# Cross attention of layer 1: scores kept with keys on partitions, so that the weights need no transposing

## The chip, the cores and the metric

The kernel runs on one core of one Trainium2 chip, as one launch. The metric is device time in microseconds (us), lower is better: the median of repeated runs. The profile below is of one further execution.

## The reference

The network is a two-layer perceiver block over x of shape (16, 64, 512), with a context of (16, 1601, 512) and a mask over the 1601 keys. Layer 0 (a similarity attention, a self attention and a mixture of experts) and what follows the cross attention in layer 1 (a differential attention with a feed-forward block, then a ternary feed-forward block with a convolution) are untouched. The changed part is the cross attention of layer 1, in float32, with 16 heads of 32:

```
q = split_heads(queries @ Wq + bq)      # queries: layernorm(x), 64 rows in each of 16 batches
k = split_heads(keys @ Wk + bk)         # keys = values = ctx, 1601 rows in each batch
v = split_heads(values @ Wv + bv)
scores = einsum('bhqd,bhkd->bhqk', q, k) / sqrt(32)
scores = where(mask, -1e15, scores)
attn = softmax(scores, axis=-1)
ctx = einsum('bhqk,bhkd->bhqd', attn, v)
return ctx @ Wo + bo
```

## The kernel before

Layer 0 comes first and takes about 866 us of the span. Layer 1 is one long loop, in l1_layer. Its outer index is the batch b (16 of them), its inner index f picks one of four groups of four heads. One pass of the inner loop is called a unit here: there are 64. A unit handles four heads of one batch as two pairs (j = 0, 1); each pair has its 2 x 64 queries together, so that a tile of scores has 128 columns or rows of queries. Eight units (two batches, b even then b odd) make a cycle, since the later work of a tile of 128 rows of x (two batches) is spread over one. The units of a cycle are named U0 to U7 in this document: U0 to U3 are f = 0 to 3 of an even batch, U4 to U7 of an odd one.

In a unit of the kernel before:

- blank tiles p (128 queries x 1601 keys, one for each pair) are filled with -1e15 by GpSimd (POOL), L1182;
- scores (L815) puts queries on partitions: the block-diagonal queries qbd are the stationary operand, 64 rows of the array for each pair j, and the projected keys kT are streamed, 384 or 449 keys to a PSUM bank. The four banks of the tag "mm" take half of the keys at a time. VectorE (DVE) copies the allowed scores over the blanks (copy_predicated, L823), with the mask as uint8;
- DVE takes the maximum of each row (L1192), and ScalarE (ACT) computes the exponential with the maximum as bias and sums it in the same instruction (L1193);
- one unit later, TensorE (PE) transposes the 2 x 13 blocks of weights (transpose_keys, L182), ACT copies them out of PSUM (L185), and attend (L833) multiplies them with the values, 52 matmuls of 32 columns x 64;
- at the end of a batch, finish transposes the sums, inverts them on DVE, spreads them over partitions by matmuls with the 0/1 tile "spread" (L852), and scales the result.

Between these stand the projections of the next unit's keys (project_k, L146: 4 matmuls for each of four chunks n, copied out of PSUM by ACT at L758 into kT) and, in units of even f, of the values (project_v, L146). Steps of the later layers are interleaved: `run(behind, ...)` takes some steps of the generator later(t) after every chunk n. Their heavy part on DVE is products (L886 a product of 128 x 1024, L887 its sum over 16), 24 of these pairs in a cycle, which fall at the end of U0 and in U1 to U3. later(t) waits on the finished cross attention of the tile before.

The program is written in this order, and each engine works through a queue of its own strictly in order; a waiting instruction holds everything behind it on its engine. A scheduler of the framework fixes the order of each queue when the kernel is built: it may move an instruction ahead of others of its engine, as far as buffers and dependences allow. Buffers: four PSUM banks "mm" in turn for scores and projections, two "tp" for transposes, two "acc"; four tiles p, so that those of one unit come free when attend of that unit is done.

## Time and profile before

| | |
|---|---|
| runs (us) | 3614.35, 3618.15, 3618.94; median 3618.15 |
| profiled execution: its time, its span | 3622.86, 3621.2 |
| span to the first score of layer 1 | about 894 us |
| the 64 units | about 894 to 3405 us |
| one cycle of eight units, in the steady part | 324.3 to 326.2 us (the first cycle, with other work interleaved, 256.9) |
| rest after the last unit (the last tile's later layers) | about 216 us |
| busy share of the span: PE, PE weight loads, DVE, ACT, POOL | 91%, 61%, 45%, 31%, 10% |

A line of the profile names a line of the kernel, an engine, an operation, out<-in, partitions x elements, and a count; then the busy time in us and the mean of one in ns. A float32 matmul stands in it as two records. The granted PE clock (PEclk) is the share of full speed that the throttle allowed. The end of a matmul's record is modelled: where matmuls follow each other, the distance between starts is the time that one costs.

### The profile page before, as it was taken

The numbers are of one execution on the slowest core, as the hardware profiler recorded it, in microseconds if no ns is written. First come the engines' busy times: TensorE is split into PE (matmuls) and PEld (weight loads), VectorE is DVE, ScalarE is ACT, GpSimd is POOL, SyncE is SP. The second block draws the span as 40 slices with busy tenths as digits, with TensorE's granted clock in tenths as the row PEclk, the third lists the DMA queues.
The fourth block names the chain that finished last, engine by engine and source line by source line (L and its number), as shares of the span: only waits on it lengthen the run. The fifth ranks groups of instructions, "written<-read, shape, count | busy, mean of one in ns | idle before, by whom it ended". The sixth has DMA issues, their size and how long they took to land. (4 is left out here: it accounts for less than half of the span.)

```text
span 3621.2 us, 49699 instructions
## 1 busy us (share of the span) xinstructions
PE 3285.8 (91%) x21116; PEld 2194.4 (61%) x21116; DVE 1639.5 (45%) x2580; ACT 1139.1 (31%) x2214; POOL 377.3 (10%) x340
## 2 busy tenths in 40 slices
PE   6898998995999999999999999999999999999815
PEld 2242445583667766767676676766667766666614
DVE  2010214214443743582566249345725744581583
ACT  1111011111333334343433433343434334343402
POOL 0000001442011010011001000100110010010000
PEclk9999998997999999999999999999999999999957
DMA  9949301596421113212311322232133113213213
GB/s 357 355 160 371 124 11 57 204 347 194 143 83 58 58 57 120 92 45 88 118 47 51 115 99 65 71 109 73 39 105 112 62 48 124 93 39 100 67 35 119
DMA packets 267374, 418.03 MB, mean 115 GB/s; under 512 B 20736, under 2 KB 164224, under 8 KB 267152
## 3 DMA queue, kind: packets, MB, share of 16 engines
q1 hardware_dynamic: 254656, 370.28, 31.1%
q0 software_dynamic: 12496, 44.57, 3.6%
q8 instruction: 166, 2.72, 0.3%
q14 instruction: 56, 0.46, 0.0%
HBM read 392.26 MB, written 22.54 MB: 115 GB/s over the span
## 5 line engine op out<-in xcount | busy, mean ns | idle before, releaser
L146 PE MATMUL ps_mm<-ctxT,x1w 128*128 128x384 f32 x1536 | 555.3, 492 | 1.9 <-DVE p L823 0.2
L146 PE MATMUL ps_mm<-x1w,ctxT 128*128 128x256 f32 x2304 | 523.7, 381 | 0.0
L146 PEld LDWEIGHTS ps_mm<-x1w,ctxT 128*128 128x128 f32 x2304 | 434.4, 190 | 79.8
L823 DVE COPY_PREDICATED p<-mk,ps_mm 128x384 f32<-128x384 uint8 (+1 forms) x512 | 270.1, 595 | 356.9 <-PE ps_mm L815 356.8
L1182 POOL MEMSET p<- 128x1601 f32 x128 | 185.9, 1454 | 1852.4 <-PE ps_tp L182 1848.7
L146 PEld LDWEIGHTS ps_mm<-ctxT,x1w 128*128 128x128 f32 x1536 | 273.1, 192 | 133.6 <-DVE p L823 7.3
L185 ACT COPY pT<-ps_tp 128x512 f32<-128x512 f32 x504 | 230.4, 503 | 356.8 <-PE ps_tp L182 356.8
L773 ACT COPY v<-ps_mm 128x256 f32<-128x256 f32 (+1 forms) x416 | 152.1, 370 | 418.6 <-PE ps_mm L146 417.9
L182 PEld LDWEIGHTS ps_tp<-ident,p 128*128 128x128 f32 (+1 forms) x1768 | 200.0, 143 | 137.2 <-issue 57.6
L182 PE MATMUL ps_tp<-ident,p 128*128 128x128 f32 (+1 forms) x1768 | 256.9, 282 | 4.8 <-ACT pT L185 1.6
L1192 DVE TENSOR_REDUCE negm<-p 128x1 f32<-128x1601 f32 x128 | 226.6, 1811 | 1.2
L146 PE MATMUL ps_mm<-x1w,ctxT_last 128*128 128x256 f32 (+1 forms) x1024 | 226.2, 379 | 0.0
L886 DVE TENSOR_TENSOR prod<-qkv 128x1024 f32<-128x1024 f32 x128 | 156.6, 1223 | 138.4 <-ACT qkv L918 134.8
L1193 ACT ACTIVATE p<-p,negm 128x1601 f32<-128x1601 f32 x128 | 208.0, 1627 | 14.3 <-DVE negm L1192 13.6
L146 PEld LDWEIGHTS ps_mm<-x1w,ctxT_last 128*128 128x128 f32 (+1 forms) x1024 | 181.2, 177 | 48.5 <-issue 12.1
L146 PE MATMUL ps_mm<-ctxT_last,x1w 128*128 128x449 f32 x512 | 206.4, 540 | 0.0
L815 PE MATMUL ps_mm<-kT,qbd 64*128 64x384 f32 x768 | 197.0, 528 | 0.1
L758 ACT ACTIVATE kT<-ps_mm,cols 128x384 f32<-128x384 f32 x192 | 109.4, 578 | 206.5 <-PE ps_mm L146 206.5
L146 PEld LDWEIGHTS ps_mm<-hT,w 128*128 128x128 f32 x1024 | 132.2, 194 | 56.1 <-ACT hid L1002 40.4
L887 DVE TENSOR_REDUCE att<-prod 128x64 f32<-128x1024 f32 x128 | 155.9, 1218 | 3.7
L146 PE MATMUL ps_mm<-uT,w 128*128 128x512 f32 (+1 forms) x512 | 150.9, 456 | 7.2 <-DMA w<-in_x_Wq_dram 5.5
L146 PE MATMUL ps_mm<-hT,w 128*128 128x128 f32 x1024 | 142.6, 284 | 2.4 <-ACT hid L1002 1.0
(290 smaller groups left out, 3809.3 us busy)
## 6 DMA issues: line engine op xcount, KB each, us to landing
ctxT<-in_ctx_T_dram SPq DMA_DIRECT2D x48, 1024.0 KB, 12.5
ck<-in_ctx_dram SPq DMA_DIRECT2D x48, 1024.0 KB, 11.8
ctxT<-in_ctx_T_dram SPq DMA_DIRECT2D x48, 768.0 KB, 4.5
w<-in_W1T_dram SPq DMA_DIRECT2D x64, 512.0 KB, 4.5
w<-in_W2T_dram SPq DMA_DIRECT2D x64, 512.0 KB, 3.7
wt<-tern SPq DMA_DIRECT2D x64, 512.0 KB, 4.3
ctxT_last<-in_ctx_T_dram SPq DMA_DIRECT2D x16, 898.0 KB, 4.8
w<-in_x_Wq_dram SPq DMA_DIRECT2D x16, 512.0 KB, 4.4
```

Of the source, the lines that this page charges most:

```text
L146: g.nc.tensor.matmul(out, lhsT=lhs(c), rhs=rhs(c), start=(c == 0), stop=(c == n - 1))
L182: g.nc.tensor.transpose(pt[:kw, j, :], p[:, k0 + j * P : k0 + j * P + kw], g.ident)
L185: (out_of or (lambda o, i: evac(g, o, i)))(pT[:kw, :blocks, :], pt[:kw, :blocks, :])
L758: nc.scalar.activation(kT, ps[:, :w], AF.Identity, bias=col(g, "x1_bk", f))
L773: nc.scalar.copy(v[:kw], ps[:kw, :256])
L815: nc.tensor.matmul(bank[:, : KC[n][1]], lhsT=qbd[ts(j, 2 * HDX), f].rearrange("p j s -> p (j s)"), rhs=kTs[b, f, n][ts(j, 2 * HDX), :], st ...
L823: nc.vector.copy_predicated(ps_[j][:, k0 : k0 + w], mk[:, k0 : k0 + w], bank[:, :w])
L886: nc.vector.tensor_tensor(pr, qv.unsqueeze(2).to_broadcast([P, CH, 32, 16]), kv, ALU.mult)
L887: nc.vector.tensor_reduce(out[:, ts(i, CH * 32)], pr.rearrange("p i j d -> p (i j) d"), AX.X, ALU.add)
L1182: nc.gpsimd.memset(p, -1e15)
L1192: nc.vector.tensor_reduce(negm, p, AX.X, ALU.max, negate=True)
L1193: nc.scalar.activation(p, p, AF.Exp, bias=negm, accum_out=sums[:, 2 * f + j : 2 * f + j + 1])
```

## The change

The scores are computed transposed. The keys kT become the stationary operand, and qbd is streamed: a block of 128 keys x 128 queries for each pair, 26 matmuls in a unit in place of 8. The first eight blocks are issued where scores stood; the other five after the first chunk of project_k. The mask is transposed to the keys' side once for each batch (allowed): PE does it in bfloat16, DVE copies it back to uint8. The copy_predicated instructions take four blocks at a time, with the mask broadcast over the two heads of a pair. The tile p is then 128 keys x 13 blocks x 128 queries, and attend uses it as it stands. The 26 transposes of a unit and their copies on ACT are gone.

The softmax now runs over partitions and blocks. DVE takes the maximum over the 13 blocks (maxima); PE transposes this 128 x 128 tile for each pair; DVE takes the maximum of each row, negated, and multiplies the identity with it (minus_max); a matmul with ones spreads these values to all partitions (weights), and DVE adds them to p; ACT computes the exponential without bias or sum. The sum over the blocks is done by POOL with five additions for each pair, and the sum over partitions by four matmuls with ones in attend, which write to the second half of the bank po. finish inverts there, and the tile spread is gone. blank now takes four memsets, as the last block is only 65 keys high.

```diff
--- before.py
+++ after.py
@@ -667,7 +666,7 @@
     nc, tc = g.nc, g.tc
     wk, wv = g.wk, g.wv
-    NP = HX // 2
+    NB = len(KT)
     with ExitStack() as es:
...
-        ptpool = pool("x1_pt", 6)
...
-        spread = one.tile([NP, 2, NC, P], F32, tag="spread", name="spread")
...
@@ -793,74 +781,139 @@
             )
             qTs[t] = qT
+        def allowed(b):
+            m8 = mpool.tile([S, S2], U8, tag="m8", name="m8")
+            nc.sync.dma_start(out=m8, in_=g.mask[b])
+            mb = mpool.tile([S, S2], BF16, tag="mb", name="mb")
+            nc.vector.tensor_scalar(mb, m8, 0.0, None, ALU.is_equal)
+            pt = g.ps.tile([P, NB, S], BF16, tag="tp", name="ps_tm", bufs=g.psbufs["tp"])
+            for k, (k0, kw) in enumerate(KT):
+                nc.tensor.transpose(pt[:kw, k, :], mb[:, ds(k0, kw)], identb[:S, :S])
+            mk = mpool.tile([P, NB, S], U8, tag="mk", name="mk", bufs=2)
+            nc.vector.tensor_copy(mk[:, : NB - 1], pt[:, : NB - 1])
+            nc.vector.tensor_copy(mk[:kw, NB - 1], pt[:kw, NB - 1])
+            return mk
         def prepare(b, qT):
-            mk = mpool.tile([P, S2], U8, tag="mk", name="mk")
-            for j in range(2):
-                nc.sync.dma_start(out=mk[ts(j, S), :], in_=g.mask[b])
-            nc.vector.tensor_scalar(mk, mk, 0.0, None, ALU.is_equal)
             qbd = spool.tile([P, NC, 2, S], F32, tag="qbd", name="qbd", bufs=2)
             for j in range(2):
                 nc.vector.tensor_scalar(
                     qbd[:, :, j, :], qT[:, :, ts(b % 2, S)], parity[:, j : j + 1], None, ALU.mult
                 )
-            return mk, qbd
-        def scores(b, f, ns, ps_, mk, qbd):
...
-                k0, w = KC[n]
+            return qbd
+        def scores(b, f, blocks, ps_, mk, qbd):
+            banks = [(k, j, mm(g)) for k in blocks[::4] for j in range(2)]
+            for n in reversed(range(len(banks) // 2)):
+                for k in blocks[4 * n : 4 * n + 4]:
+                    c = min(k // 3, len(KC) - 1)
+                    at, kw = k * P - KC[c][0], KT[k][1]
+                    for j in range(2):
+                        nc.tensor.matmul(
+                            banks[2 * n + j][2][:kw, ts(k % 4, P)],
+                            lhsT=kTs[b, f, c][ts(j, 2 * HDX), ds(at, kw)],
+                            rhs=qbd[ts(j, 2 * HDX), f].rearrange("p j s -> p (j s)"),
+                            start=True, stop=True,
+                        )
+            for k, j, bank in banks:
+                n = min(4, NB - k)
+                rows = KT[k][1]
                 nc.vector.copy_predicated(
-                    ps_[j][:, k0 : k0 + w], mk[:, k0 : k0 + w], bank[:, :w]
-                )
...
-                for r in reversed(range(4)):
+                    ps_[j][:rows, k : k + n, :].rearrange("p k (h s) -> p k h s", h=2),
+                    mk[:rows, k : k + n, :].unsqueeze(2).to_broadcast([rows, n, 2, S]),
+                    bank[:rows, : n * P].rearrange("p (k h s) -> p k h s", k=n, h=2),
+                )
+        def blank():
+            p = ppool.tile([P, NB, P], F32, tag="p", name="p")
+            nc.gpsimd.memset(p[:, : NB - 1], -1e15)
+            nc.gpsimd.memset(p[: P // 2, NB - 1], -1e15)
+            nc.gpsimd.memset(p[P // 2 :, NB - 1], -FMAX)
+            nc.gpsimd.memset(p[P // 2 : KT[-1][1], NB - 1], -1e15)
+            return p
+        def maxima(ps_):
+            mx = spool.tile([P, 2, P], F32, tag="mx", name="mx")
+            for j, p in enumerate(ps_):
+                nc.vector.tensor_reduce(
+                    mx[:, j, :], p.rearrange("p k x -> p x k"), AX.X, ALU.max
+                )
+            return mx
+        def minus_max(mx):
+            pt = mm(g, tag="tp")[:, : 2 * P].rearrange("p (j x) -> p j x", j=2)
+            for j in range(2):
+                nc.tensor.transpose(pt[:, j, :], mx[:, j, :], g.ident)
+            negm = small.tile([P, 2], F32, tag="negm", name="negm")
+            nc.vector.tensor_reduce(negm, pt, AX.X, ALU.max, negate=True)
+            dg = spool.tile([P, 2, P], F32, tag="mx", name="dgm")
+            for j in range(2):
+                nc.vector.tensor_scalar(dg[:, j, :], g.ident, negm[:, j : j + 1], None, ALU.mult)
+            return dg
+        def weights(ps_, dg):
+            pb = mm(g, tag="tp")
+            nc.tensor.matmul(
+                pb[:, : 2 * P], lhsT=g.ones, rhs=dg.rearrange("p j x -> p (j x)"),
+                start=True, stop=True,
+            )
+            H = NB // 2
+            sums = []
+            for j, p in enumerate(ps_):
+                nc.vector.tensor_tensor(
+                    p, p, pb[:, ts(j, P)].unsqueeze(1).to_broadcast([P, NB, P]), ALU.add
+                )
+                nc.scalar.activation(p, p, AF.Exp)
+                s = spool.tile([P, H, P], F32, tag="sum", name="sum", bufs=3)
+                nc.gpsimd.tensor_tensor(s, p[:, :H], p[:, H : 2 * H], ALU.add)
+                nc.gpsimd.tensor_tensor(s[:, :3], s[:, :3], s[:, 3:], ALU.add)
+                for q in (s[:, 1], s[:, 2], p[:, NB - 1]):
+                    nc.gpsimd.tensor_tensor(s[:, 0], s[:, 0], q, ALU.add)
+                sums.append(s[:, 0])
+            return sums
+        def attend(b, f, ps_, po, sums):
+            for k in range(NB):
+                kw = KT[k][1]
+                for r in range(4):
                     nc.tensor.matmul(
                         po[ts(r, HDX), ts(f, S)],
                         lhsT=vs[b, f // 2, k][:, ts(4 * (f % 2) + r, HDX)],
-                        rhs=pTs[r // 2][k][:, ts(r % 2, S)],
-                        start=(k == len(KT) - 1), stop=(k == 0),
+                        rhs=ps_[r // 2][:kw, k, ts(r % 2, S)],
+                        start=(k == 0), stop=(k == NB - 1),
                     )
+            for r in range(4):
+                nc.tensor.matmul(
+                    po[ts(r, HDX), ts(NC + f, S)], lhsT=g.ones[:, :HDX],
+                    rhs=sums[r // 2][:, ts(r % 2, S)], start=True, stop=True,
+                )
         otile, qTs = {}, {}
-        def finish(b, po, rs8):
+        def finish(b, po):
             t, hb = divmod(b, 2)
-            pt = mm(g, tag="tp")
-            nc.tensor.transpose(pt[:NP, :P], rs8, g.ident)
...
-            nc.scalar.copy(rb.rearrange("p f s -> p (f s)"), pr[:, : NC * S])
+            rb = spool.tile([P, NC * S], F32, tag="rb", name="rb")
+            nc.vector.reciprocal(rb, po[:, NC * S :])
             if hb == 0:
                 otile[t] = spool.tile([P, NC, P], F32, tag="oT", name="oT")
             oT = otile[t]
             nc.vector.tensor_tensor(
                 oT[:, :, ts(hb, S)],
-                po[:, : NC * S].rearrange("p (f s) -> p f s", f=NC), rb, ALU.mult,
+                po[:, : NC * S].rearrange("p (f s) -> p f s", f=NC),
+                rb.rearrange("p (f s) -> p f s", f=NC), ALU.mult,
             )
             if hb == 0:
                 return
@@ -1172,32 +1225,13 @@
             project_k(0, 0, n)
         pending = None
         behind, asked = ternary_weights(), iter(())
+        mk_next = allowed(0)
         for b in range(B):
-            mk, qbd = prepare(b, qTs[b // 2])
+            mk, qbd = mk_next, prepare(b, qTs[b // 2])
             for f in range(NC):
                 bk, fk = divmod(b * NC + f + 1, NC)
-                ps_ = []
-                for j in range(2):
...
-                    ]
+                ps_ = [blank() for j in range(2)]
+                scores(b, f, range(8), ps_, mk, qbd)
                 before = pending
                 if b % 2 == 1 and f == 0 and b + 1 < B:
                     asked = queries(b // 2 + 1)
@@ -1205,17 +1239,24 @@
                     if bk < B:
                         project_k(bk, fk, n)
                     if n == 0:
+                        scores(b, f, range(8, NB), ps_, mk, qbd)
                         if before is not None:
-                            attend(*before[:2], pTs, before[3])
+                            attend(*before)
                             if f == 0:
-                                finish(b - 1, *before[3:])
+                                finish(b - 1, before[3])
                         if f == 0:
                             po = mm(g, tag="acc")
                             if b % 2 == 0 and b > 0:
                                 behind = later(b // 2 - 1)
-                        pending = (b, f, ps_, po, sums)
+                        mx = maxima(ps_)
+                    if n == 2:
+                        dg = minus_max(mx)
+                        if f == 2 and b + 1 < B:
+                            mk_next = allowed(b + 1)
                     if f % 2 == 0:
                         project_v(b, f // 2, n)
+                    if n == 3:
+                        pending = (b, f, ps_, po, weights(ps_, dg))
                     run(behind, 1 if f % 2 == 1 or b % 2 + f == 0 and n < 2 else 3 + f // 2)
                     if n == 3:
                         run(asked, 1)
@@ -1223,9 +1264,8 @@
                     load_ctx(b + 1)
             if b % 2 == 1:
                 run(behind)
-        pTs = [transpose_keys(g, ptpool, p) for p in pending[2]]
-        attend(*pending[:2], pTs, pending[3])
-        finish(B - 1, *pending[3:])
+        attend(*pending)
+        finish(B - 1, pending[3])
         run(later(NT - 1))
```

## The prediction, made before the changed kernel was run

> **What bounds the kernel now.** I read first the busy shares of the page, then the same shares unit by unit, then what PE waits for, then one unit in order of time. The page says that PE is the bound, and its rows by slices say that this holds from about 894 to 3405 us, where the 64 units lie, while DVE swings between one tenth and nine:
>
> ```profile
> PE 3285.8 (91%) x21116; PEld 2194.4 (61%) x21116; DVE 1639.5 (45%) x2580; ACT 1139.1 (31%) x2214; POOL 377.3 (10%) x340
> ...
> PE   6898998995999999999999999999999999999815
> ...
> DVE  2010214214443743582566249345725744581583
> ```
>
> The windows of one steady cycle, U0 to U7, each from a unit's first scores to the next unit's, show where DVE is dense (the columns are the busy us of PE, PEld, DVE, ACT and POOL, then the granted clock, the DMA share and GB/s):
>
> ```profile
> 2450.00:2510.90 60.90, 60.18 (x380) 46.13 (x377) 27.23 (x38) 19.09 (x40) 4.15 (x3) 1.00 0.31 92
> 2510.90:2532.90 22.00, 20.85 (x183) 12.48 (x182) 21.69 (x22) 10.42 (x17) 2.87 (x2) 1.00 0.13 46
> 2532.90:2579.10 46.20, 43.70 (x293) 32.28 (x290) 43.04 (x43) 16.08 (x32) 4.07 (x4) 1.00 0.23 69
> 2579.10:2599.50 20.40, 19.06 (x159) 12.03 (x160) 17.30 (x27) 9.54 (x16) 2.87 (x2) 0.83 0.06 18
> 2599.50:2669.30 69.80, 68.54 (x434) 50.55 (x433) 14.67 (x27) 23.75 (x51) 6.74 (x5) 1.00 0.24 75
> 2669.30:2701.40 32.10, 31.61 (x237) 19.34 (x237) 9.88 (x16) 13.09 (x24) 2.87 (x2) 1.00 0.42 132
> 2701.40:2752.70 51.30, 49.45 (x382) 38.50 (x381) 26.65 (x60) 26.53 (x55) 3.08 (x2) 1.00 0.29 98
> 2752.70:2776.20 23.50, 22.27 (x197) 13.59 (x196) 15.97 (x31) 10.57 (x18) 2.87 (x2) 1.00 0.23 76
> ```
>
> U1 to U3 hold most of the products. DVE is busy there for 82.0 of 88.6 us: PE and DVE are both full. Elsewhere DVE has room. What PE waits for in the steady part is small, and all of it stands at this attention:
>
> ```profile
> PE ps_acc L833 <- ACT pT L185: 22.6, 35, 1.3
> PE ps_mm L815 <- DVE p L823: 21.9, 23, 2.0
> ```
>
> **What PE gets back.** This is PE in the first part of U1 (start, us, then the instruction; x counts records, two to a float32 matmul, one to a transpose):
>
> ```profile
> 2510.95 1.67 PE L815 MATMUL ps_mm<-kT,qbd 64*128 64x384 f32 x8
> 2512.55 0.66 PE L182 MATMUL ps_tp<-ident,p 128*128 128x128 f32 x4
> ...
> 2517.73 1.04 PE L182 MATMUL ps_tp<-ident,p 128*128 128x128 f32 x8
> 2518.60 0.81 PE L146 MATMUL ps_mm<-ctxT,x1w 128*128 128x384 f32 x2
> 2519.25 0.71 PE L182 MATMUL ps_tp<-ident,p 128*128 128x128 f32 x5
> 2519.79 0.49 PE L146 MATMUL ps_mm<-ctxT,x1w 128*128 128x384 f32 x1
> ```
>
> From 2510.95 to 2519.79 are 8.84 us; two stretches of projection inside take 0.75 and 0.65, so scores and transposes cost 7.4 us with their waits. attend adds 1.6 us and a wait of 0.5. finish has 16 records of L852 at 0.125 (29.9 us for 240) and a transpose for each batch, 0.5 us a unit. Sum 10.0 us.
>
> New on PE in a unit: 52 records of scores, 128 wide. A 128-wide record on all rows costs 0.11 us (L146 hT,w: 8 in 1.05 us less the modelled end). The two pairs sit on different halves of the rows; the old scores cost 0.56 of the same width on all rows (8 records of 384 in 1.67 against 2.74 us, ends taken off). So 0.061 each, 3.2 us; bounds 2.9 and 5.7 (no overlap), taken 3.2, as weight loads of the halves already come four in 0.3 us. attend: 56 matmuls at 0.032 (104 records in 1.66 us), 1.8. Two transposes 0.2; the ones matmul, two 256-wide records at 0.22, 0.45; the mask, 13 bfloat16 transposes near 0.1 (their weight loads: 98 ns), 0.3 a unit. Sum 6.0. PE gets back 4.0 us a unit, 256 us in 64, if nothing waits. ACT loses the copies of L185, about 4 us a unit, which only PE's waits felt. SP carries one mask transfer a batch for two, issued earlier; nothing queues behind it.
>
> **What DVE pays, a unit.** Two additions of 1664 elements: 512 from PSUM cost 0.691 us (L1106), 1024 cost 1.223 (L886), so 1.04 ns an element and 1.89 us each, 3.8. The maxima: contiguous like L1192 they cost 1.88; but L1137, which reads across a stride as here, took 1.061 us for 512 against 0.668 contiguous (L1081). The 0.39 belongs to its 128 results (then 2.3 us) or to its 512 reads (3.2): I take 2.5, over 1.81 before, +1.4 for two. The second maximum 0.42 (L1142 and 128 elements more), the two diagonals 0.54 (L1064), the copies 4.3 against 4.1. Sum +6.3 us; the mask adds 1.1 a batch and now falls wholly in U2, 2.2 there.
>
> **Where it waits.** The order built for each queue is known.
>
> (a) *DVE-bound stretch.* In U1 to U3, 82.0 + 3 x 6.3 + 2.2 = 103.1 us, less half a pair of products now ahead of U1 (1.2), is 101.9 us of DVE against 88.6 us of wall: +13.3 a cycle with DVE never idle, +20 if its old 6.6 us of idleness stay. The static order puts one or two pairs of products between the maxima and the diagonals, so PE cannot run ahead.
>
> (b) *Additions before copies.* At U3/U4 and U5/U6 (U1/U2 and U2/U3 lie in (a)), PE's ones matmul is directly followed by the 16 first scores, which fill all four banks, and then by project_k, which needs a bank. The copy that frees it queues behind both additions: 0.2 + 3.8 + 0.63 less 1.95 of scores is 2.7 us of PE idle. At the other four boundaries 3.4 us or more of other matmuls stand in between. If that cover goes, 2.7 each.
>
> (c) *A bank through ACT.* The last five blocks need the bank that project_k(0) has just filled: ACT's 0.58 (L758) and the hand-over, 0.8 us in each unit outside (a).
>
> (d) *Sums on POOL.* 1536 elements for a pair at 2.46 ns (L988: 512 in 1.263; L944: 256 in 0.620), 3.8 us, two pairs 7.6, memsets about 4.2: 12 us, inside every unit. They end 11.3 us after the ones matmul, when PE has come 11 us on: nothing, but any slowing is PE's.
>
> (e) *U7*: the second maximum queues behind the ternary stage's scaling on DVE, 2 us.
>
> The Trainium skill speaks against the change here: "SBUF — State Buffer", Who interferes with whom, says that a DVE instruction with two SBUF inputs and a POOL instruction that reads SBUF exclude each other for a whole instruction. The row cannot tell: L886 lasted 1204 to 1229 ns throughout, beside a POOL that mostly only wrote. By the rule, some third of 24 products meets an addition and waits 0.6 us: 5 us a cycle, in (a), where it counts. By the row, 0. I take 5; without it the end is 35 us lower.
>
> And the clock. "TensorE: Matmul & The Clock Gate", HAM oscillation, warns of idle gaps above about 3.4 us. The trace is stricter: U3 above, with waits of 1.99 and 0.57 us, was granted 0.83, and such U3 last 19.6 to 20.4 us against 18.8 at 0.91. I price each gap of (b) at 1.2 us by the row; by the rule it would be 0, and the end 20 us lower.
>
> **The sum.** A steady cycle: U0 -3.2; U1 to U3 +13.3; U4 and U6 -4.0 + 2.7 + 0.8 = -0.5 each; U5 -3.2; U7 -1.2; clock +2.4; lock +5: +12, seven times +85. The first cycle (ternary work, U1 and U3 at 17.6 of 23.9 and 18.7 of 19.5 us of DVE): U1 +1, U3 +6, U5 and U7 +1.6 each, the even ones -0.5: +8. The tail trades transposes for the longer softmax: 0. Together +93. The profiled execution took 3622.86 us (span 3621.2), 4.7 above the median, so on the median of the runs: 3618 + 93, **3710 us**.
>
> **The rivals.**
>
> *Products give way, faster.* DVE is idle for 34 us in U0 and 55 in U4. If the products really slide there, U1 to U3 lose nothing but PE's gain: they break even once they grow by less than 8.6 us a cycle (the sum of the other five units) in place of 13.3 plus lock and clock. At zero growth, -8.6 x 7 and some 20 in the first: 3540 us; with no wait at all, 3362. Against it: the queue's order is fixed, with the pairs where they were. Chance 0.25.
>
> *No overlap of the row halves.* Scores at 5.7 us: 2.5 x 40 units outside DVE's hold, +100: 3810. Against it is the ratio 0.56. Chance 0.10.
>
> *DVE and POOL heavier.* Maxima 3.2 us (+4 a cycle), DVE's old idleness kept (+6.7), sums late by a lock on both sides: 3800. Chance 0.10.
>
> *It cancels.* Gain and waits within 0.2%, about what this measurement can tell from no change: 3615. Chance 0.05.
>
> **How the numbers follow.** The likeliest case has 0.50, its own range 3640 to 3790. Faster is the first rival and 0.02 of the likeliest, 0.27; same 0.05; slower 0.68. The range leaves out the lower part of the first rival and the upper tails: 3520 to 3830.
>
> **What would show it.** Right: L182 gone from the units; score records near 0.06 us apart; additions near 1.9 us; a cycle near 337 us, with U1 and U3 longer, U0 and U5 shorter; PE waiting at project_k for the copies, with a lower clock. Wrong: U1 to U3 not longer than 88.6 us; PE's share of the cycle still 97%; or waits of PE for POOL's sums of several us.

## The result and the profile after

The change makes the kernel slower: 3722.36 us, median of four runs (3718.62 to 3729.11), against 3616.32 us for the kernel before on the same chip. The ratio is 1.0295, with a 95% interval of 1.0276 to 1.0314. The forecast was 3710 us.

The profiled execution took 3719.31 us with a span of 3717.5, 96.3 us more span than before. (The medians lie 106 us apart: the profiled execution of the kernel before was 6.5 us above its median, this one 3.1 below.) Cut at the same instruction in each unit (the start of the unit's first maximum), those 96.3 us lie here: 0.4 ahead of the first unit, 28.3 in the first cycle (256.9 before, 285.2 after), 64.4 in the other seven (6.5 to 11.3 us each), 3.2 in the tail (216.8 before, 220.0 after).

The page's first part and its slices, of the changed kernel:

```profile
PE 3202.4 (86%) x22460; PEld 2182.1 (59%) x22460; DVE 2103.6 (57%) x2928; ACT 886.0 (24%) x1548; POOL 1024.6 (28%) x1357
...
PE   6898998995889989989988998999899989989715
...
DVE  2110214214865865794778469567846865794673
```

PE has 83 us less work in its records and DVE 464 us more; yet DVE's share of the span is only 57%. PE's row, one solid block of nines before, has eights all through the loop. The windows of one steady cycle, U0 to U7, each from 7.4 us ahead of the unit's first maximum as in the prediction's table (there that was the first scores), with the columns of the prediction's table (us, then busy time of PE, PEld, DVE, ACT and POOL, granted clock, DMA share, GB/s):

```profile
2516.60:2576.20 59.60, 56.48 (x402) 44.67 (x398) 37.43 (x45) 17.92 (x31) 25.58 (x29) 1.00 0.31 96
2576.20:2602.20 26.00, 19.92 (x206) 12.98 (x207) 25.90 (x28) 5.04 (x6) 5.03 (x9) 0.93 0.04 15
2602.20:2651.40 49.20, 42.18 (x318) 31.83 (x316) 44.23 (x45) 10.86 (x21) 13.91 (x21) 0.92 0.22 70
2651.40:2678.40 27.00, 21.12 (x216) 13.34 (x217) 25.50 (x26) 6.46 (x7) 15.45 (x21) 0.94 0.01 2
2678.40:2742.40 64.00, 62.69 (x403) 47.33 (x403) 25.08 (x42) 19.50 (x41) 22.19 (x29) 0.98 0.28 88
2742.40:2773.50 31.10, 30.14 (x272) 19.66 (x271) 15.80 (x20) 7.57 (x13) 3.89 (x8) 1.00 0.39 126
2773.50:2827.10 53.60, 48.87 (x397) 38.73 (x399) 37.68 (x72) 22.94 (x44) 12.49 (x18) 0.97 0.32 106
2827.10:2851.20 24.10, 21.47 (x221) 13.13 (x219) 20.98 (x36) 6.54 (x9) 12.26 (x19) 1.00 0.19 61
```

| unit | before | after | difference | predicted |
|---|---|---|---|---|
| U0 | 60.9 | 59.6 | -1.3 | -3.2 |
| U1 to U3 | 88.6 | 102.2 | +13.6 | +13.3, and 5 for the lock |
| U4, U5 | 101.9 | 95.1 | -6.8 | -3.7, and 1.2 for the clock |
| U6, U7 | 74.8 | 77.7 | +2.9 | -1.7, and 1.2 for the clock |
| cycle | 326.2 | 334.6 | +8.4 | +12 |

U1 to U3 carry the loss. DVE is busy for 95.6 of their 102.2 us (82.0 of 88.6 before), and at first sight step (a) is confirmed. What PE waits for in the loop and the drain behind it (us in total, times, longest) tells more:

```profile
PE ps_acc L892 <- ACT p L876: 77.6, 33, 5.2
PE ps_acc L899 <- POOL sum L881: 71.5, 46, 3.0
PE ps_mm L146 <- DVE p L826: 36.3, 36, 2.4
PE ps_tp L866 <- DVE dgm L860: 22.9, 13, 2.1
```

The exponentials, the sums and the banks come behind the matmul with ones; only the diagonals (22.9 us) lie ahead of it. Here is the end of U1 on PE, in order of time (start, us, then the instruction):

```profile
2595.09 0.70 PE L866 MATMUL ps_tp<-dgm,ones 128*128 128x256 f32 x2 [2.14 <-DVE dgm L860]
2595.72 3.38 PE L817 MATMUL ps_mm<-qbd,kT 64*128 64x128 f32 x32
2600.97 0.30 PE L892 MATMUL ps_acc<-p,v 128*32 128x64 f32 x4 [1.88 <-ACT p L876]
...
2601.71 4.23 PE L146 MATMUL ps_mm<-ctxT,x1w 128*128 128x384 f32 x8 [0.43 <-DVE p L826]
...
2610.94 0.31 PE L899 MATMUL ps_acc<-sum,ones 128*32 128x64 f32 x4 [1.52 <-POOL sum L881]
...
2643.34 2.06 PE L817 MATMUL ps_mm<-qbd,kT 64*128 64x128 f32 x32
```

and the same boundary on DVE:

```profile
2594.56 0.48 DVE L860 TENSOR_SCALAR dgm<-ident,negm 128x128 f32<-128x128 f32 x2
2594.95 1.21 DVE L940 TENSOR_REDUCE att<-prod 128x64 f32<-128x1024 f32 x1
2596.19 1.23 DVE L939 TENSOR_TENSOR prod<-qkv 128x1024 f32<-128x1024 f32 x1
2597.34 3.68 DVE L873 TENSOR_TENSOR p<-p,ps_tp 128x1664 f32<-128x1664 f32 x2
2600.93 2.58 DVE L826 COPY_PREDICATED p<-mk,ps_mm 128x512 f32<-128x512 uint8 x4
```

PE has the ones matmul done by 2595.7. DVE first finishes a product, then adds for 3.7 us, then copies. PE's next instructions are two matmuls of attend, which the scheduler put ahead of project_k: they need the exponential behind the first addition, and project_k needs the bank behind both. After the gap the same eight records of projection that otherwise take 2.74 us take 4.23, and the first scores took 3.38 us in place of the 2.06 they take at 2643.34. The granted clock says why:

```profile
2592.90:2595.10 2.20, 0.06 (x2) 0.01 (x1) 2.20 (x6) 0.64 (x1) 0.00 (x0) 1.00 0.00 0
2596.20:2599.60 3.40, 2.90 (x30) 2.60 (x26) 3.40 (x3) 0.27 (x1) 0.00 (x0) 0.50 0.00 0
2603.00:2606.40 3.40, 3.40 (x10) 1.54 (x9) 1.60 (x2) 0.36 (x1) 3.16 (x5) 0.50 0.00 0
```

In the first of these windows PE all but stands; in the other two, behind the gaps, it has half its clock.

### The profile page after: what moved, and what is told of

It is laid out like the page before. It is cut to its first block, busy times and chain, and to the rows that moved or that the text cites. A ratio compares the mean times of both kernels' runs of the same rounds, so it can differ in the third digit from the quotient of the medians.

```text
span 3717.5 us, 53532 instructions
## 1 busy us (share of the span) xinstructions
PE 3202.4 (86%) x22460; PEld 2182.1 (59%) x22460; DVE 2103.6 (57%) x2928; ACT 886.0 (24%) x1548; POOL 1024.6 (28%) x1357
## 4 chain that ended last, share of the span: by engine, by line
PE 54%; DVE 30%; DMA 6%; POOL 5%; ACT 4%; issue 2%; SPq 0%; POOLq 0%; ACTq 0%; DVEq 0%
PE ps_mm L146 36%; PE ps_acc L146 7%; DVE mx L845 6%; DVE prod L939 6%; DVE att L940 4%; PE ps_acc L1062 3%; DVE p L873 3%; DVE p L826 3%; DMA ctxT<-in_ctx_T_dram 3%; DMA ck<-in_ctx_dram 2%; POOL sum L878 2%; PE ps_mm L817 2%; DVE o L940 2%; POOL sum L881 2%; PE ps_acc L282 1%
## 5 line engine op out<-in xcount | busy, mean ns | idle before, releaser
L878 POOL TENSOR_TENSOR sum<-p 128x768 f32<-128x768 f32 x128 | 244.7, 1912 | 1126.7 <-ACT p L876 1126.7
L826 DVE COPY_PREDICATED p<-mk,ps_mm 128x512 f32<-128x512 uint8 (+1 forms) x512 | 285.1, 619 | 294.9 <-PE ps_mm L817 275.0
L845 DVE TENSOR_REDUCE mx<-p 128x128 f32<-128x1664 f32 x128 | 379.7, 2996 | 0.0
L873 DVE TENSOR_TENSOR p<-p,ps_tp 128x1664 f32<-128x1664 f32 x128 | 235.6, 1882 | 126.9 <-PE ps_tp L866 126.9
L835 POOL MEMSET p<- 128x1536 f32 x128 | 177.4, 1386 | 264.7 <-PE ps_acc L899 255.0
L876 ACT ACTIVATE p<-p 128x1664 f32<-128x1664 f32 x128 | 201.8, 1587 | 135.6 <-DVE p L873 135.0
L817 PE MATMUL ps_mm<-qbd,kT 64*128 64x128 f32 x2304 | 206.4, 294 | 10.3 <-DVE p L826 3.7
L817 PEld LDWEIGHTS ps_mm<-qbd,kT 64*128 64x128 f32 x2304 | 172.0, 198 | 43.2 <-ACT kT L746 17.9
L892 PE MATMUL ps_acc<-p,v 128*32 128x64 f32 x6656 | 119.1, 222 | 79.7 <-ACT p L876 79.6
L939 DVE TENSOR_TENSOR prod<-qkv 128x1024 f32<-128x1024 f32 x128 | 158.6, 1239 | 44.4 <-ACT qkv L971 41.3
L892 PEld LDWEIGHTS ps_acc<-p,v 128*32 128x32 f32 x6656 | 102.0, 111 | 95.5 <-ACT p L876 87.4
```

Source lines behind the costliest of these rows:

```text
L817: nc.tensor.matmul(banks[2 * n + j][2][:kw, ts(k % 4, P)], lhsT=kTs[b, f, c][ts(j, 2 * HDX), ds(at, kw)], rhs=qbd[ts(j, 2 * HDX), f].rearr ...
L826: nc.vector.copy_predicated(ps_[j][:rows, k : k + n, :].rearrange("p k (h s) -> p k h s", h=2), mk[:rows, k : k + n, :].unsqueeze(2).to_br ...
L835: nc.gpsimd.memset(p[:, : NB - 1], -1e15)
L845: nc.vector.tensor_reduce(mx[:, j, :], p.rearrange("p k x -> p x k"), AX.X, ALU.max)
L873: nc.vector.tensor_tensor(p, p, pb[:, ts(j, P)].unsqueeze(1).to_broadcast([P, NB, P]), ALU.add)
L876: nc.scalar.activation(p, p, AF.Exp)
```

## The experiments

Each ratio is to the kernel before on the same chip (its median there was 3613 to 3620 us). "U1 to U3" and the cycles are read from DVE's maxima as above.

| kernel | us | ratio to before (95%) | first cycle | steady cycle | U1 to U3 |
|---|---|---|---|---|---|
| before | 3616.3 | 1 | 256.9 | 324.3 to 326.2 | 87 to 89 |
| changed | 3722.4 | 1.0295 (1.0276 to 1.0314) | 285.2 | 331.1 to 336.7 | 99 to 105 |
| half_max | 3688.3 | 1.0206 (1.0186 to 1.0225) | 284.6 | 331.1 | 97.9 |
| late_sums | 3714.2 | 1.0277 (1.0256 to 1.0297) | 273.3 | 334.4 to 337.5 | 104 |
| project_first | 3762.8 | 1.0406 (1.0388 to 1.0423) | 285.6 | 338.2 to 340.9 | 99 to 105 |
| spread | 3724.2 | 1.0296 (1.0278 to 1.0314) | 280.1 | 334.6 to 337.4 | 99 to 103 |
| before_noprod | 3515.2 | 0.9717 (0.9701 to 0.9733) | 256.5 | 318.2 | 80.6 |
| after_noprod | 3639.2 | 1.0063 (1.0047 to 1.0080) | 285.0 | 331.1 | 91.5 |
| no_max | 3463.6 | 0.9575 (0.9559 to 0.9591) | 254.1 | 304.0 | not cut alike |
| late_attend | 3783.8 | 1.0468 (1.0450 to 1.0485) | 277.1 | 344.7 | 106 |
| no_add | 3650.6 | 1.0099 (1.0082 to 1.0116) | 255.5 | 331.0 | 97.4 |
| defer | 3695.2 | 1.0221 (1.0203 to 1.0238) | 259.4 | 334.4 to 337.5 | 100 to 102 |
| before_load | 3683.3 | 1.0179 (1.0162 to 1.0196) | 258.3 | 332.5 to 336.4 | 94.4 |
| no_add_noprod | 3453.9 | 0.9546 (0.9530 to 0.9563) | 254.9 | 309.5 to 311.1 | 77.6 |

### First round: is it DVE's load, the sums, or the boundary?

**half_max.**

```diff
-                    mx[:, j, :], p.rearrange("p k x -> p x k"), AX.X, ALU.max
+                    mx[:, j, :], p[:, 6:NB].rearrange("p k x -> p x k"), AX.X, ALU.max
```

> The changed kernel with its maxima taken over the last 7 of the 13 blocks of keys (the other six are left out of the maximum, which is only a shift under the exponential). Takes 3.0 x 6/13 = 1.4 us from each maximum, 2.8 us of VectorE a unit, and nothing from any other engine. Theory 'VectorE holds U1 to U3' (step a): those three units shorten by about 8 us a cycle, 8 cycles, some 3660 us. Rival 'what PE waits for is the length of the chain additions, exponentials, POOL sums, whatever VectorE's load': maxima lie before that chain with 15 us of room, so under 10 us, 3712 to 3722.

3688.3 us: half of what the load theory wanted. U1 and U2 hardly moved (25.6 and 48.6 us), U3 lost 3. Of the 34 us saved, some 21 are in the seven later cycles, the rest ahead of the first unit and in the tail. In the row of its maxima, 896 elements take 1692 ns against 2996 for 1664: 1.7 ns an element, so the stride costs on the reads.

**late_sums.**

```diff
+            if f == NC - 1:
+                sum_up(b, f, ps_, po, sums)
+
+        def sum_up(b, f, ps_, po, sums):
...
+                    if n == 1 and before is not None and f > 0:
+                        sum_up(*before)
```

> The changed kernel with the four matmuls of the sums (L899) moved behind project_k(1) of the next unit where f is not 0. The work is the same. Theory 'PE's 71.5 us at L899 are lost to POOL's sums' (step d wrong): three units of four lose their wait, about -50 us, 3670. Rival 'in U1 to U3 VectorE decides, and a wait taken away there comes back at the copies or the diagonals': only U5 to U7 gain, some 1.5 us each, about -30, 3690. If the sums cost nothing, 3720.

3714.2 us. The waits of PE after it:

```profile
PE ps_acc L892 <- ACT p L876: 97.5, 33, 7.1
PE ps_mm L146 <- DVE p L826: 35.8, 36, 2.4
PE ps_tp L866 <- DVE dgm L860: 32.1, 15, 2.1
PE ps_tp L1124 <- DVE dg L1122: 15.8, 7, 2.4
PE ps_acc L904 <- POOL sum L881: 13.6, 12, 2.3
```

The wait for sums fell from 71.5 to 13.6 us, and most of the same time came back: exponentials +20, diagonals +9, the ternary stage's scale (dg) +12. The steady cycle did not shorten; only the first did (273.3 us). That PE waits somewhere for 71.5 us did not mean that removing this wait gains them.

**project_first.**

```diff
+                if bk < B:
+                    project_k(bk, fk, 0)
                 scores(b, f, range(8), ps_, mk, qbd)
...
-                    if bk < B:
+                    if bk < B and n > 0:
```

> The changed kernel with project_k(0) of a unit ahead of its first 16 scores in place of behind them. Theory of step b: PE then has 2.1 us of matmuls and 2 us of scores under the additions, the wait at U3/U4 and U5/U6 shrinks by 2 us or more each, and the lower clock behind it goes: about -40 us, 3680. Rival 'the wait is only moved, to the last scores, which need the same banks': 3715 to 3725.

3762.8 us, 40 slower. The rival's mechanism is there, and costs more than it expected: the exponentials' wait fell from 77.6 to 23.3 us, but the sums' rose from 71.5 to 98.0, and the last scores now wait 35.5 us for their banks.

**spread.**

```diff
-                    run(behind, 1 if f % 2 == 1 or b % 2 + f == 0 and n < 2 else 3 + f // 2)
+                    run(behind, 1 if f % 2 == 1 or b % 2 + f == 0 and n < 2 else
+                        3 if b % 2 + f == 0 else 2 if b % 2 == 0 else 5 if f == 0 else 4)
```

> The changed kernel with the later stage's steps handed out differently: U2 takes 2 steps a chunk in place of 4, U4 takes 5 in place of 3, nothing else differs. Up to 8 pairs of products (2.45 us each, 19.6 us of VectorE) move out of U2 and U3 into U4, where VectorE was busy for 25 of 64 us. Theory 'VectorE holds U1 to U3': these lose up to the 14 us a cycle that they are longer than before, seven cycles, 3620 to 3640. Rival 'the chain's length and POOL decide': no gain, 3715 to 3730.

3724.2 us, and no test: the scheduler put the products almost where they had been. In U2 DVE was busy for 43 to 45 us, against 44.2, and 8 pairs of products began there, as in the changed kernel. The program's order hands out the steps, but does not fix where they run.

### Second round: take the load away, take the chain away

**before_noprod and after_noprod.** In both, one multiplication of 64 columns takes the place of each pair of products:

```diff
-                pr = prod.tile([P, CH, 32, 16], F32, tag="prod", name="prod")
                 qv = q[:, ts(i, CH), :]
-                nc.vector.tensor_tensor(pr, qv.unsqueeze(2).to_broadcast([P, CH, 32, 16]), kv, ALU.mult)
-                nc.vector.tensor_reduce(
-                    out[:, ts(i, CH * 32)], pr.rearrange("p i j d -> p (i j) d"), AX.X, ALU.add
+                nc.vector.tensor_tensor(
+                    out[:, ts(i, CH * 32)].rearrange("p (i j) -> p i j", i=CH),
+                    qv[:, :, 0:1].to_broadcast([P, CH, 32]), kv[:, :, :, 0], ALU.mult,
                 )
```

> The kernel before with the products (L886, L887) left out: in place of each pair stands one multiplication of 64 columns, so that the attention of the later stage is wrong. Takes 24 pairs of 2.45 us, 59 us of VectorE, from each cycle and from the tail behind the last unit. The tail is serial there, so about 50 us go; in the units PE is the bound and little more goes: 3540 to 3570.

> The changed kernel with the same products left out. Theory 'VectorE's load holds U1 to U3' (step a): without the products VectorE has room everywhere, and the change costs no more than its waits at the unit boundaries: 3520 to 3560, within 20 us of the kernel before without products. Theory 'the length of the chain from the matmul with ones over additions and exponential to attend, and POOL's sums, decides': VectorE's load matters little, and the changed kernel stays 70 to 100 us behind the other, 3610 to 3660.

3515.2 and 3639.2 us, 124 us apart, where the two full kernels are 106 apart. So the products are not needed for the loss: with DVE idle for 43 of U1 to U3's 91.5 us, the change still costs 11 us there and 12.9 in a cycle. Step (a) as the sole cause falls. before_noprod itself ended 25 us under its expectation: beside the tail, U1 to U3 lost some 7 us in each steady cycle (80.6 in place of 87 to 89), so DVE's load already cost something there before the change. What PE waits for in after_noprod:

```profile
PE ps_acc L899 <- POOL sum L881: 84.3, 55, 2.5
PE ps_mm L146 <- DVE p L826: 68.2, 36, 3.8
PE ps_acc L892 <- ACT p L876: 35.3, 22, 2.9
```

These three are 188 us, and the wait for diagonals is gone. This is the boundary alone: additions, then copies, exponentials and sums, with no product near.

**no_max.** Maxima, minus_max, the ones matmul and the additions are left out:

```diff
-                nc.vector.tensor_tensor(
-                    p, p, pb[:, ts(j, P)].unsqueeze(1).to_broadcast([P, NB, P]), ALU.add
-                )
...
-                        mx = maxima(ps_)
...
-                        dg = minus_max(mx)
```

> The changed kernel without any shift under the exponential: maxima, their transposes, the second maximum, the diagonals, the matmul with ones and the additions are left out. Takes 10.7 us of VectorE and 0.65 us of PE from each unit, and the exponential no longer waits for additions. Both theories expect it under 3520, since load and length go together; what tells is PE's wait for POOL's sums (71.5 us in the changed kernel), which vanishes if it came from late exponentials and stays if POOL itself is too slow.

3463.6 us, 259 below the changed kernel, and PE's wait for sums is gone from the list altogether, though POOL's additions are as slow as before (L870 here, 1991 ns, against 1912 for L878 of the changed kernel). The sums were late because the exponentials were. This kernel is faster than both, but nothing bounds the exponent in it, so it replaces neither.

**late_attend.**

```diff
-        vpool = pool("x1_v", 15)
+        vpool = pool("x1_v", 18)
...
                         scores(b, f, range(8, NB), ps_, mk, qbd)
+                        mx = maxima(ps_)
+                    if n == 1:
                         if before is not None:
                             attend(*before)
...
-                        mx = maxima(ps_)
```

> The changed kernel with attend (and finish) behind project_k(1) in place of project_k(0), and three more buffers for values so that nothing waits for these; the work is the same. Between the matmul with ones and attend stand then 2.7 us more of projection. Theory 'length of the chain': PE's waits of 77.6 us for exponentials and 71.5 us for sums shrink by most of it, and the lower clock behind them goes: 3610 to 3650. Theory 'VectorE's load': the waits come back at the diagonals and copies, 3690 to 3720.

3783.8 us, slower by 61; both theories missed. Sums no longer wait, but the exponentials' wait is 93.0 us: the scheduler still put the first two matmuls of attend ahead of project_k(0), where they had been. The rest of attend came late. Two waits of 35 us each grew up: for the later stage's normalised rows, which depend on the finished batch, and at the last scores for their banks (5.9 in the changed kernel).

### Third round: one link of the chain, and a new order

**no_add.**

```diff
-                nc.vector.tensor_tensor(
-                    p, p, pb[:, ts(j, P)].unsqueeze(1).to_broadcast([P, NB, P]), ALU.add
-                )
```

> The changed kernel with only the two additions of the negated maximum (L873) left out; maxima, diagonals and the matmul with ones stay, so that VectorE loses 3.8 of the 10.7 us a unit that the run without any shift took away. Theory 'the additions stand ahead of the copies and of the exponential' (step b, at every boundary): nearly the whole gain of that run comes back, less the 0.65 us of PE a unit that stays, 42 us: 3500 to 3530. Theory 'VectorE's load': 3.8/10.7 of that run's 259 us, 92: 3630.

3650.6 us, between the two, and nearer to the 3630 of the load theory than to the other's 3500 to 3530. The first cycle is 255.5 us in place of 285.2: its whole loss was the additions. But the steady cycle shortened by 3.4 only, because other waits took over:

```profile
PE ps_tp L866 <- DVE dgm L860: 70.5, 22, 4.9
PE ps_mm L146 <- DVE p L826: 57.7, 17, 6.8
PE ps_tp L1116 <- DVE dg L1114: 32.9, 7, 7.5
```

Exponentials (9.6 us, as L889) and sums (none) no longer wait. Now PE waits for DVE's queue: diagonals, copies and scales with products ahead of them. Part of this is a cost that the edit brought in. With the additions gone, the diagonals and products of DVE meet POOL's sums more often, and take longer. First the changed kernel's row, then those of no_add:

```profile
L860 DVE TENSOR_SCALAR dgm<-ident,negm 128x128 f32<-128x128 f32 x128 | 30.5, 280 | 0.9
...
L936 DVE TENSOR_TENSOR prod<-qkv 128x1024 f32<-128x1024 f32 x128 | 171.7, 1341 | 105.4 <-ACT qkv L968 102.5
L860 DVE TENSOR_SCALAR dgm<-ident,negm 128x128 f32<-128x128 f32 x128 | 57.8, 491 | 1.0
```

In the trace of no_add the 65 diagonals that overlap in time with an operation of two inputs on POOL took 697 ns in the mean, the 63 others 279; of the products 49 took 1638, the 143 others 1221. That is some 47 us of DVE in the run, so this run is not the removal of one link alone.

**defer.** Units of odd f hand their additions to the next unit, behind its scores:

```diff
-                s = spool.tile([P, H, P], F32, tag="sum", name="sum", bufs=3)
+                s = spool.tile([P, H, P], F32, tag="sum", name="sum", bufs=4)
...
                         scores(b, f, range(8, NB), ps_, mk, qbd)
...
+                            if f % 2 == 1:
+                                attend(*before)
+                                sum_up(*before)
+                            else:
+                                before += (weights(*late),)
...
+                        elif before is not None:
+                            attend(*before)
...
+                    pending = (b, f, ps_, po, weights(ps_, dg))
+                    project_v(b, f // 2, 3)
```

> The changed kernel with the same work in another order. In units of odd f the matmul with ones and the additions wait until the next unit's scores are done, and attend of them stands behind project_k(2) there; in units of even f the projections of values stand behind all those of keys, the matmul with ones ahead of the last 7 us of them, and the sums follow 5 us of projection after attend. So additions never stand between scores and their copies. Theory of the boundaries: most of the 31 us of waits a cycle and the lower clock behind them go, and the 4 us a unit of PE that the change gives back show: 3480 to 3560, under the kernel before. Theory of load: VectorE stays as full, 3680 to 3720.

3695.2 us, as the theory of load had it (3680 to 3720). The first cycle is 259.4, the steady one unchanged, and one wait above all has taken the place of the others:

```profile
PE ps_mm L146 <- DVE p L826: 119.3, 38, 8.6
```

The waits for exponentials (3.4 us) and sums (3.1) are gone, as intended; in their place PE waits for copies that stand in DVE's queue behind other work, and for the later stages' rows (37.7) and scales (23.5).

### Fourth round: two limits?

**before_load.** The kernel before, with DVE work that nobody waits for:

```diff
+                    for w in (S2, 1185):
+                        extra = small.tile([P, 1], F32, tag="extra", name="extra")
+                        nc.vector.tensor_reduce(extra, p[:, :w], AX.X, ALU.max)
```

> The kernel before with VectorE work added that nobody waits for: behind each exponential two more maxima over p (1601 and 1185 elements, 1.81 and 1.34 us by L1192's row), 6.3 us a unit, as much as the prediction's sum for the changed kernel; the results are dropped. Theory of step a, VectorE's load alone holds U1 to U3: a cycle grows by 12 to 19 us as predicted for the change, 3700 to 3740. Theory that only the chain between the matmul with ones and the next scores costs: VectorE's load without a wait of PE behind it costs under 20 us, 3616 to 3636.

3683.3 us: +63, a cycle 9.3 us longer, U1 to U3 6 to 7, the first cycle only 1.4. Both theories missed. Load alone does slow the steady cycles, and it hardly slows the first, where there are no products. But the load did not land as it was meant to. These are its U1 to U3, each from the unit's first maximum:

```profile
2224.21:2245.88 21.67, 21.09 (x187) 12.95 (x186) 21.57 (x23) 11.35 (x19) 2.98 (x3) 1.00 0.01 2
2245.88:2293.76 47.88, 44.99 (x276) 31.82 (x275) 43.12 (x43) 13.74 (x29) 4.07 (x4) 0.93 0.22 69
2293.76:2318.56 24.80, 24.80 (x192) 14.90 (x192) 23.69 (x24) 11.05 (x20) 4.19 (x3) 0.94 0.03 9
```

DVE is busy for 88.4 of 94.4 us, 6.4 more than before and not the 19 that were added: other work moved out, two pairs of products among it. So the run does not show that load costs less than step (a) said; 6.4 us of DVE's work went with 5.8 us of wall. How it reaches PE is open, since PE's idle time there did not grow (3.5 us, 5.0 before) and its records became longer.

**no_add_noprod.** Both edits at once.

> The changed kernel with both the two additions and the products left out, each of which alone gave only 3.4 us in a steady cycle. Theory of two limits beside each other (the additions' chain at the unit boundaries, and a VectorE queue full of products ahead of the diagonals and copies, where the one takes over when the other is gone): together they give far more than their sum, a steady cycle near 295 us and 3340 to 3420 in all. Rival, the two simply add up and something else holds the cycle: 3722 less 83 less 72, 3550 to 3585.

3453.9 us. The windows of U1 to U3 (from each unit's first maximum) show PE nearly full again, at full clock:

```profile
2142.60:2161.91 19.31, 17.54 (x198) 10.99 (x190) 14.94 (x19) 6.51 (x7) 12.62 (x18) 1.00 0.01 2
2161.91:2202.51 40.60, 40.43 (x333) 31.18 (x325) 13.18 (x18) 10.07 (x19) 12.00 (x18) 1.00 0.27 84
2202.51:2220.22 17.71, 17.53 (x216) 11.32 (x208) 12.14 (x14) 5.34 (x6) 12.09 (x18) 1.00 0.01 2
```

Apart, the two edits shortened U1 to U3 by 4.5 us (no_add) and about 10 (after_noprod), the steady cycle by some 3.4 each. Together it is 24 us in U1 to U3 and 23 to 25 in the cycle. That is more than their sum. The whole time lies between the theory of two limits (3340 to 3420) and its rival (3550 to 3585), and the cycle stops near 310, not 295: PE still waits 4.7 us a cycle for the ternary stage's scale and 3.1 for the finished batch. With both gone, the rest of the change runs 61 us below the old kernel without products: so much it could give there if its additions cost nothing. And without products the additions are shown to be the cause: from after_noprod to no_add_noprod they alone take a cycle from 331 to 310, where the kernel before without products has 318.

With products the apart gains understate each edit, because each also brought something new. no_add has the dearer diagonals and products above. In after_noprod U1 to U3 became 10.5 us shorter, but the other five units 7 us longer (239.5 us against 232.4), with waits of 3.8 us for copies in U0 and 3.5 us for exponentials and sums in U4, where the changed kernel has none: the order built is another.

## Why the prediction was right, and where it was not

The total came out 12 us from the measurement, and a cycle at 334.6 against 337. Slower was foreseen for the right two reasons, DVE-bound units and additions ahead of copies. That the number fits so well is in part luck: the seven later cycles lost 64.4 us where the sum had 85, the first lost 28.3 where it had 8, and the tail 3.2 where it had 0. Errors of 21 and 23 us cancel.

**What PE gets back: too large.** PE's work can be read where little disturbs it: 310.9 us of PE a cycle in before_noprod, at a clock of 1.00, and 295.2 in no_add_noprod, at 1.00 but for U7 (0.94), so 15.7 less. The prediction's 32 us a cycle counted the old waits with it, some 10 us, so 22 in the same terms. The pace of the scores was right for the first sixteen: 32 records in 2.06 us, 0.061 after the modelled end. The other ten are slower: with their change of chunks and banks they take 1.9 us from start to start, where 20 x 0.061 gave 1.2. That alone is 5 to 6 us a cycle.

**The account of the cycle.** PE's work -15.7 us. Its busy time exceeds that work by 7.7 us in the changed kernel (302.9 less 295.2), by 4.8 before (315.7 less 310.9): +2.9, the lower clock and hand-overs between banks; the prediction had 2.4. Idle time of PE 31.7 against 10.5: +21.2. Sum +8.4, as measured. In the prediction's terms -22, +2.4 and +31.6 made +12: a gain and a loss both too large.

**(a), the DVE-bound stretch: the size fits, by two errors that cancel, and the cause was not the only one.** U1 to U3 grew by 13.6 us, for 13.3. The step had 101.9 us of DVE's work there and no idle time; measured are 95.6 us of work and 6.6 of idle time, as much as before. Where the step kept the old idle time it had +20. And emptying DVE (after_noprod against before_noprod) leaves 11 us of loss. The runs speak for two limits in the same units: the chain from the matmul with ones to the next copies, and DVE's queue, in which products stand ahead of diagonals and copies. How the 8.4 us of a full cycle divide between them the runs don't say.

**(b), additions before copies: mechanism right, place wrong.** The step priced 2.7 us at two boundaries of eight, and gave U1/U2 and U2/U3 to (a). In the steady cycle PE waits for exponentials or copies at four: 3.6 us in U1, 6.0 in U2, 3.7 in U3, 2.0 in U6, together 15.3 in place of 5.4. The scheduler made it worse than the step saw: two matmuls of attend were put ahead of project_k. In the first cycle it is the whole loss: +28.3 us where the sum had +8, and no_add brings that cycle back to 255.5. The first cycle has no products: its DVE is busy for 176 of 285 us, and the prediction, which looked for load, priced it low.

**(d), sums on POOL: 0 predicted, 71.5 us of waits.** The sums start when the exponential ends, and the step took that to be soon: in U1 they end 15.8 us after the ones matmul (2595.1 to 2610.9), where it had 11.3. POOL was also slower than estimated: the 128-wide additions took 565 ns in the mean, where the rate of the 256-wide row gave 0.32 us. Yet late_sums gained 8 us, and no_add and no_max have no such wait. It is the end of the chain in (b), not a limit of its own.

**The lock.** The Trainium skill's rule on DVE and POOL ("SBUF — State Buffer", Who interferes with whom) was priced at 5 us a cycle on DVE. There the changed kernel pays little: the products' rows say 1239 and 1259 ns after, 1223 before, 4 to 5 us in the whole run. POOL pays more. Groups of the changed kernel (count, busy us, mean ns):

```profile
L845 DVE TENSOR_REDUCE mx<-p 128x128 f32<-128x1664 f32 x128 | 379.7, 2996 | 0.0
...
L939 DVE TENSOR_TENSOR prod<-qkv 128x1024 f32<-128x1024 f32 x128 | 158.6, 1239 | 44.4 <-ACT qkv L971 41.3
...
L881 POOL TENSOR_TENSOR sum<-sum 128x128 f32<-128x128 f32 x256 | 144.6, 565 | 20.1
```

In one stretch of POOL's queue the same addition of 384 takes 1.00 us while DVE copies from PSUM or reduces, and 1.88 us while a product and a copy run:

```profile
2602.97 1.00 POOL L879 TENSOR_TENSOR sum<-sum 128x384 f32<-128x384 f32 x1
...
2607.40 1.88 POOL L879 TENSOR_TENSOR sum<-sum 128x384 f32<-128x384 f32 x1
```

Counted by overlap in time over the whole trace, the 44 additions of 128 that met a product took 1046 ns in the mean, the 340 others 466; for those of 384 it is 1568 (19) against 1023, for those of 768 2544 (14) against 1834. POOL lost some 46 us in the run so, and its delay joined (d). The 49 products that met a two-input operation of POOL took 1315 ns, four beside a memset 1224, and the other 139 took 1222. In no_add it is DVE that pays more (1638 ns for such a product). So the two hold each other up, as the page says; that a lock on a port does it was not tested here.

**Single terms.** The additions took 1.882 us (predicted 1.89), the second maximum 418 ns, the diagonals 280 each (0.54 for two predicted). The maxima took 2.996 us, near the upper bound of 3.2 and not the 2.5 taken: half_max shows that each strided read costs. U4 and U5 gained 6.8 us in place of 3.7 less 1.2 for the clock, with almost no wait there. U6 lost 2.3, mostly its waits for sums (3.1) and copies (2.0), where (b) had 2.7. The 0.8 us a unit of (c) are hardly there as a wait: PE is idle for 10.3 us before all its scores of the run, 0.2 a unit; what the bank costs beyond that would lie in the 1.9 us of the last ten.

**The rivals.** "Products give way" did not happen: of the 18 pairs that began in U1 to U3 of a cycle before, 17 or 18 do so after, though some slid from U2 to U3. "No overlap of the row halves" is excluded by the 2.06 us. "DVE and POOL heavier" was right in its terms for maxima and sums, but the time stayed under its 3800, as the gains elsewhere show.

## What to carry to other kernels

Work that moves from an idle engine's copies into the chain between two stages of the bound engine cost twice here: the chain's length is paid where the in-order queue has nothing else to issue, and the added load is paid where that engine's queue is full. Here removing one gained 3 us a cycle and removing both 24. Before reading such a run, look whether the edit did only what was meant: added load moved elsewhere in before_load, and no_add made what it left dearer. A wait that the profile totals at 70 us can be worth 8, as late_sums shows: ask first what it waits behind, and which wait would end next. And cut the span into cycles before explaining it: over a quarter of this loss lay in the one cycle that had none of the work that the prediction blamed.

## What the runs showed of the hardware

- A maximum over a stride of 128 float32 elements took 2996 ns for 1664 reads and 1692 ns for 896, 1.7 ns a read; contiguous (L1192 before) 1601 reads took 1811 ns, 1.1 a read.
- Behind gaps of about 2 us PE ran the same matmuls up to 1.6 times as long (first scores 3.38 us against 2.06, a projection of eight records 4.23 against 2.74), with a granted clock of 0.50 for 3.4 us at a time. In no_add_noprod, whose longest gap in U1 to U3 is 1.4 us, the clock of those units is 1.00.
- An addition on POOL that met a product of DVE took 1.4 to 2.2 times as long (1046 ns against 466, 1568 against 1023, 2544 against 1834). The products that met one lengthened from 1222 to 1315 ns, in no_add from 1221 to 1638, and the diagonals there from 279 to 697.
